# New planned times for every step of a two-layer graph kernel (graph attention, then graph convolution)

## The chip, the core and the metric

The kernel runs on one core of a Trainium2 chip. The metric is device time in microseconds (us), the median of the runs; smaller is better. TensorE is called PE, VectorE DVE, ScalarE ACT, GpSimd POOL, and SyncE, which here only issues DMAs, SP.

## What is computed

`x` is 32 batches of 512 rows (C) by 1024 columns (N), all float32; `adj` is a 512 x 512 matrix.

```python
h = maximum(layernorm(x), 0)                 # over the 1024 columns
q, k = wq . h, wk . h                        # one number per column
scores[m, n] = leaky(q[n] + k[m], 0.01)
att = softmax(scores, over n)
agg[c, m] = sum_n h[c, n] att[m, n]
x = x + relu(adj @ agg + bm)                 # layer 0
h = maximum(layernorm(x), 0)
x = x + (adj * adj).T @ h + bias             # layer 1
```

## The kernel before, in words

Attention is not done as a 1024 x 1024 product. The score of a pair is the sum of two numbers bent at zero, so for a given m every n whose q lies above a threshold gets one exponential factor, and every n below it another. The kernel ranks the 1024 columns by q, writes the rows of V = (adj @ h).T to DRAM in the order of rank, forms running sums over the sorted rows from both ends, and then each column m looks up where it stands in the order and picks three rows with one gather.

The work of one batch is cut into about 180 **steps**, each a small function that issues a few instructions:

- `load`, `stats0`, `norm0`, `slopes0`, `relu0`: x in four tiles of 128 x 1024; bn_stats on DVE, square root and relu on ACT.
- `scores` (PE, L349, 32-column products), ACT copies the result and DMAs it to DRAM; `row` (L360) reads it back broadcast to all partitions; `columns` (L365, L370) transposes it.
- `value` (L454): eight steps of four 128 x 512 float32 products each (two PE instructions per product); `spread` copies V to SBUF.
- `rank` (DVE, L391, L396, L400), `to_rows`: ranks and row numbers; `scatter` (POOL, L467) writes V's rows to DRAM in order of rank; `fetch` (SP, L484) reads them back sorted.
- `lower` (ACT, L407), `from_rows` (DVE, L437 to L447): where each column m stands.
- `weights` (ACT, L493, L496), `later` (DVE, L504, L508), `totals` (PE, L516, L517, then the copy of the denominators, L521), `stationary` (POOL, L527): weights of the sorted rows and the triangular matrices of the running sums.
- `scan` and `sums`, nine each: one step of the running sums. The two directions run in the two column halves of the array as 128 x 64 products (L543); in the fifth step (i = 4) both directions read the same block of rows, and one 128 x 128 product does it (L540). `sums` (ACT) copies two carry rows into the next blocks (L552, L553), which the next `scan` needs, then the sum itself (L555, L556), and SP stores it (L558, L559).
- `gather` (POOL, L564), `excess`, `divide`, `weigh` (ACT, L589), `combine` (DVE, 16 steps, L593): the three picked rows become one. `turn0`, `turn1` (L600): PE transposes back, four steps each, and DVE adds to x (L602).
- `stats1`, `norm1`, `slopes1`, `relu1`, `lift`: layer norm of layer 1. `propagate` (L607): eight steps of four products; `finish` (L615) adds on DVE, and SP stores the output.

What sets the order is a table. `PLAN` gives each step of a batch a time; batch b's are shifted by b * T. `FIRST` and `LAST` give the first five and last five batches a shift and a stretch for each kind of step. All steps of all batches are sorted by these times and issued in that order, so each engine has one fixed list that it runs from the front; what an engine waits for, everything behind it on that engine waits for too. The times are used for nothing else.

```python
times = PLAN[name]
mean = sum(times) / len(times)
...
t = s.b * T + t + shift + stretch * (t - mean)
steps.append((t, len(steps), f, (s, *lead, *(args[n] if args else (n,)))))
...
steps.sort(key=lambda e: e[:2])
with tc.manual_schedule():
    for _, _, f, args in steps:
        f(*args)
```

Buffers that bind neighbouring batches: 8 PSUM banks for all products, one buffer for the gathered rows (of 788 KB a gather step), five for the sorted rows (three a batch), two for sums on their way to DRAM, seven each for x and y tiles, eight for V.

Of the kernel before, what the change touches and what calls it, by code (L numbers as in the profile page):

```python
# [27 lines left out]
    "adjacency": (-107.86,),  # L28
    "biases": (73.25,),
    "columns": (2.54,),  # L30
    "combine": (
        293.1, 294, 295.37, 296.17, 294.24, 294.54, 295.16, 296.42, 294.48,
        294.66, 293.61, 295.28, 294.87, 296.68, 296.01, 296.52,
    ),
    "compare_mask": (-77.25,),
    "divide": (278.91,),
    "excess": (272.83,),
    "factors": (28.83,),
    "fetch": (74.87,),
    "finish": (357.8, 362.86, 376.29, 376.42, 388.63, 415.81, 401.13, 417.85),  # L40
    "from_rows": (89.36,),
    "gather": (250.12, 258.6, 255.35, 261.49, 268.91, 253.59, 258.29, 256.1),
    "later": (82.34,),
    "lift": (341.79, 343.89, 354.9, 347.45),
    "load": (-125.04, -82.54, -104.22, -58.22),
    "lower": (26.37, 18.82, 14.83, 28.33, 13.66, 12.67, 46.5, 36.18),
    "masks": (-12.78,),
    "norm0": (-27.69,),
    "norm1": (323.91,),
    "pads": (1.15,),  # L50
    "propagate": (347.57, 348.71, 350.13, 365.41, 372.81, 382.23, 382.61, 392.3),
    "rank": (16.85, 14.2, 18.53, 15.82, 17.42, 21.57, 23.3, 23.64),
    "reload": (275.48, 285.03, 274.13, 289.84),
    "relu0": (-17.18, -15.69, -15.67, -14.84),
    "relu1": (334.79, 335.4, 335.54, 338.3),
    "row": (1.98,),
    "scan": (89.28, 94.78, 102.87, 122.08, 139.17, 152.12, 172.91, 183.19, 200.42),
    "scatter": (39.55, 42.53, 43.86, 40.7, 49.58, 45.37, 44.59, 45.6),
    "scores": (-1.83,),
    "slopes0": (-22.22,),  # L60
    "slopes1": (324.32,),
    "spread": (10.78, 16.46, 5.24, 10.37, 28.25, 25.74, 19.08, 20.35),
    "square": (53.38,),
    "stationary": (83.36, 116.24, 162.19),
    "stats0": (-63.29, -60.88, -63.05, -41.14),
    "stats1": (318.79, 319.93, 319.41, 319.38),
    "sums": (89.92, 97.06, 115.14, 127.32, 141.99, 156.22, 174.86, 189.46, 207.26),
    "to_rows": (23, 29.08),
    "totals": (88.21,),
    "turn0": (303.69, 304.68, 304.05, 304.98),  # L70
    "turn1": (312.19, 312.02, 311.8, 312.15),
    "turn_adjacency": (-39.9,),
    "value": (3.89, 14.52, -1.07, 4.1, 20.69, 18.74, 15.77, 15.86),
    "weigh": (286.66, 289.32, 286.94, 289.3, 287.24, 286.87, 287.56, 291.05),
    "weights": (79,),
}
FIRST = {
    "columns": ((-37.98, 0), (-10.89, 0), (-8.73, 0), (-1.59, 0), (-5.53, 0)),
    "combine": ((-1.47, -0.283), (2.11, 0.074), (6.02, -0.446), (-3.46, 1.643), (-3.02, -0.662)),
    "divide": ((0.43, 0), (-4.84, 0), (5.31, 0), (-0.36, 0), (-5, 0)),  # L80
    "excess": ((6.36, 0), (0.71, 0), (9.39, 0), (2.63, 0), (1.02, 0)),
    "factors": ((14.45, 0), (42.49, 0), (37.13, 0), (-13.47, 0), (3.3, 0)),
    "fetch": ((-0.33, 0), (-9.12, 0), (-3.14, 0), (-6.37, 0), (-4.73, 0)),
    "finish": ((0.35, -0.506), (-4.34, -0.255), (-1.3, 0.166), (-13.48, -0.751), (-1, -0.145)),
    "from_rows": ((-17.73, 0), (122.52, 0), (-12.48, 0), (-3.68, 0), (39.28, 0)),
    "gather": ((-3.91, 0.337), (8.03, -0.392), (-0.23, 0.924), (1.48, -0.818), (-10.72, 0.312)),
    "later": ((-6.32, 0), (-2.49, 0), (-5.11, 0), (-3.44, 0), (5.07, 0)),
    "lift": ((5.78, 0.249), (-7.64, -0.77), (14.78, 1.406), (9.87, -0.096), (12.09, 1.113)),
    "load": ((-114.53, -0.719), (-41.9, -0.581), (-61.5, -0.134), (-67.36, 0.974), (-10.03, 0.381)),
    "lower": ((-4.18, -0.847), (-10.86, -0.761), (3.36, -0.598), (31.38, 0.125), (27.64, -0.444)),  # L90
    "norm0": ((-48.85, 0), (-42.24, 0), (-15.97, 0), (-23.37, 0), (-5.52, 0)),
    "norm1": ((-4.55, 0), (0.86, 0), (5.16, 0), (-3.3, 0), (2.66, 0)),
    "propagate": ((3.18, -0.698), (0.66, -0.203), (-2.02, -0.096), (-5.59, -0.325), (1.62, -0.11)),
    "rank": ((-4.4, 0.497), (1.55, -0.098), (-9.21, 1.126), (4.42, 0.365), (7.2, -0.023)),
    "reload": ((2.37, 0.404), (2.84, 0.512), (6.15, -0.047), (4.83, 0.053), (5.08, 0.729)),
    "relu0": ((-52.67, -0.811), (-32.9, 0.887), (-5.05, 1.412), (-5.92, -0.277), (0.27, -0.952)),
    "relu1": ((4.34, 0.844), (-4.2, 0.375), (9.88, -0.496), (1.58, 0.346), (-1.74, -0.782)),
    "row": ((-2.93, 0), (-19.24, 0), (-8.82, 0), (3.92, 0), (-1.39, 0)),
    "scan": ((-8.07, -0.009), (-4.12, 0.027), (-4.42, -0.075), (-2.52, 0.062), (-0.12, -0.002)),
    "scatter": ((19.59, 0.356), (0.39, -0.164), (-11.93, -0.276), (15.6, -0.115), (8.6, 0.613)),  # L100
    "scores": ((-48.13, 0), (-16.76, 0), (-5.07, 0), (-5.89, 0), (-6.97, 0)),
    "slopes0": ((-51.56, 0), (-32.21, 0), (-9.48, 0), (-3.65, 0), (3.28, 0)),
    "slopes1": ((3.12, 0), (1.34, 0), (13.39, 0), (3.58, 0), (5.29, 0)),
    "spread": ((3.65, -0.128), (-4.12, 0.811), (6.73, -0.135), (3.45, 0.185), (7.08, 1.002)),
    "stationary": ((-16.55, -0.278), (-1, 0.017), (-1.03, 0.007), (-4.23, -0.058), (4.88, -0.025)),
    "stats0": ((-86.5, 0.491), (-55.52, 0.533), (-26.5, 0.735), (-39.6, 0.274), (-0.81, 0.405)),
    "stats1": ((-2.32, 0.867), (-1.78, -0.548), (-2.88, 0.916), (-1.4, -0.748), (0.94, 0.179)),
    "sums": ((-4.03, -0.009), (-3.78, 0.04), (-3.01, -0.086), (-3.05, 0.043), (0.68, 0.024)),
    "to_rows": ((-6.46, 0.165), (-1.64, -0.568), (-5.7, -0.361), (5.62, -0.493), (8.82, -0.906)),
    "totals": ((-7.21, 0), (-4.95, 0), (-6.35, 0), (-3.7, 0), (-0, 0)),  # L110
    "turn0": ((1.54, 1.026), (5.01, 1.316), (7.07, -0.842), (11.23, 1.597), (7.25, 0.74)),
    "turn1": ((-5.63, 2.282), (4.23, 0.277), (-3.42, -0.878), (-9.56, -0.462), (0.94, 1.931)),
    "value": ((-14.35, 0.282), (-16.49, 0.638), (-1.63, 0.411), (-4.93, 0.45), (-4.23, 0.018)),
    "weigh": ((-1.72, 0.361), (-2.31, -0.775), (10.15, 0.018), (-5.33, 0.803), (-1.65, 0.186)),
    "weights": ((-3.94, 0), (-0.72, 0), (-2.63, 0), (-0.65, 0), (3.83, 0)),
}
LAST = {
    "columns": ((4.26, 0), (-3.03, 0), (2.37, 0), (-0.77, 0), (3.86, 0)),
    "combine": ((164.15, 0.268), (7.89, -0.595), (-1.54, 0.851), (5.2, 1.047), (1.56, -0.96)),
    "divide": ((162.11, 0), (3.32, 0), (-8.28, 0), (1.71, 0), (-3.58, 0)),  # L120
    "excess": ((127.64, 0), (-3.09, 0), (-3.12, 0), (2.67, 0), (0.92, 0)),
    "factors": ((-11.15, 0), (-18.33, 0), (1.07, 0), (-11.1, 0), (-11.56, 0)),
    "fetch": ((-1.81, 0), (-1.04, 0), (-0.37, 0), (-0.32, 0), (-3.1, 0)),
    "finish": ((699.4, -0.546), (150.27, -0.075), (20.88, 0.53), (4.22, 0.22), (6.11, 0.071)),
    "from_rows": ((13.84, 0), (-28.23, 0), (48.43, 0), (-17.87, 0), (17.41, 0)),
    "gather": ((88.35, 0.017), (-13.92, -0.31), (-9.45, 0.61), (-5.67, 0.718), (-2.02, 0.573)),
    "later": ((7.83, 0), (2.55, 0), (2.21, 0), (-1.95, 0), (-0.28, 0)),
    "lift": ((585.22, -0.837), (120.6, 0.105), (1.56, -0.183), (-6.91, -0.419), (9.05, -0.044)),
    "load": ((1.51, 0.156), (-2.49, 0.009), (4.84, -0.047), (9.16, -0.437), (7.85, -0.154)),
    "lower": ((9.16, 0.14), (-5.44, 0.016), (-5.91, -0.205), (-2.69, 0.118), (-12.14, -0.652)),  # L130
    "norm0": ((-2.04, 0), (-6.51, 0), (-2.65, 0), (-11.04, 0), (5.36, 0)),
    "norm1": ((418.29, 0), (27.36, 0), (-0.04, 0), (-2.45, 0), (1.02, 0)),
    "propagate": ((526.78, -0.74), (151.44, 0.764), (12.38, 0.445), (9.65, 0.206), (11.26, 0.117)),
    "rank": ((4.79, 0.609), (3.43, 0.076), (-8.9, -0.909), (-5.02, -0.932), (1.67, 0.09)),
    "reload": ((184.29, -0.585), (23.97, -0.873), (-3.56, 0.841), (1.54, 0.226), (-3.06, -0.231)),
# [27 lines left out]
def kernel(  # L163
# [457 lines left out]
    T = 80.4  # L621
# [77 lines left out]
```

## Time and profile before

| what | number |
|---|---|
| median of 3 runs (lowest to highest) | 2385.05 us (2382.75 to 2387.69) |
| the profiled execution | 2390.79 us |
| its span, first to last instruction | 2389.1 us |
| mean granted clock of PE | 0.985 |
| DMA traffic | 643.45 MB, 269 GB/s |
| start of `scores` of batches 0, 1, 2, 3, 4, 5, 6, 7 | 14.3, 53.1, 105.9, 158.9, 219.0, 293.2, 370.6, 441.3 us |
| start of `scores` of batches 28, 29, 30, 31 | 1929.5, 2004.8, 2076.9, 2140.5 us |
| from one start to the next, batches 10 to 26 | 70.5 to 71.1 us |

How to read the views: the page gives each engine's busy time and its share of the span, and rows of 40 digits, the busy tenths in 40 equal slices. The waits list who waited for whom: total, number, longest. The timeline lists instructions in order of time: start, duration, engine, line, operation, written and read tiles, and in brackets the engine's idle time before it and what ended it. A 128 x 512 product of PE is two instructions that start 0.43 us apart.

### The profile page before, as it was taken

What the parts mean: (1) busy time and instruction counts of PE and PEld (TensorE: products, weight loads), DVE (VectorE), ACT (ScalarE), POOL (GpSimd) and SP (SyncE); (2) the same over time, 40 slices, a digit from 0 to 9 for tenths busy, and PEclk for the clock granted to TensorE, in tenths of its full rate; (3) what the DMA queues carried; (4) which work ended last, traced back from release to release, by engine and by line L of the source; (5) the groups of instructions that cost most, each with busy time, mean ns of one, the idle gap of its engine ahead of it and who ended that gap; (6) DMA issues with size and microseconds to landing.
All of it is one profiled execution on the core that took longest, in us unless ns stands there. A gap on an engine that the chain in (4) does not pass through costs nothing.

```text
span 2389.1 us, 28172 instructions
## 1 busy us (share of the span) xinstructions
PE 2298.7 (96%) x7568; PEld 1016.2 (43%) x7568; DVE 1957.4 (82%) x5008; ACT 1589.4 (67%) x2878; POOL 719.5 (30%) x973
## 2 busy tenths in 40 slices
PE   7787999999999999999999999999999999999897
PEld 3233434444444444444444444444444444444343
DVE  6457978788988888988888898888898878889675
ACT  4576666766776766776676677676676856676450
POOL 2233323232332233233223233223323233223310
PEclk9898999999999999999999999999999999999898
DMA  7679887988988998988998888899998888988872
GB/s 231 154 188 279 275 286 256 302 256 269 300 284 284 289 293 258 290 294 268 293 305 261 272 291 285 285 289 282 273 281 277 281 279 250 290 267 282 290 294 87
DMA packets 206895, 643.45 MB, mean 269 GB/s; under 512 B 29120, under 2 KB 29248, under 8 KB 206736
## 3 DMA queue, kind: packets, MB, share of 16 engines
q1 hardware_dynamic: 142944, 355.74, 52.3%
q0 software_dynamic: 57344, 268.99, 30.9%
q10 hardware_dynamic: 6448, 16.92, 2.2%
q8 instruction: 61, 1.00, 0.2%
q14 instruction: 98, 0.80, 0.1%
HBM read 429.94 MB, written 211.60 MB: 269 GB/s over the span
## 4 chain that ended last, share of the span: by engine, by line
PE 84%; DMA 7%; DVE 4%; ACT 3%; issue 1%; SPq 1%; POOL 0%; ACTq 0%; DVEq 0%; POOLq 0%
PE pg L607 35%; PE pv L454 31%; PE sc L543 10%; PE tr L600 4%; DMA vs<-td 3%; PE pq L349 2%; DMA td<-t 2%; PE sc L540 1%; DVE g L593 1%; DVE st L319 1%; DMA qd<-qr 1%; DVE junk L396 1%; DMA wqk<-in_L_gnn_wk_dram 1%; DMA g<-td,idg 1%; SPq L484 0%
## 5 line engine op out<-in xcount | busy, mean ns | idle before, releaser
L607 PE MATMUL pg<-h,wsq 128*128 128x512 f32 x2048 | 908.4, 597 | 12.1 <-ACT h L337 11.9
L454 PE MATMUL pv<-wmT,x 128*128 128x512 f32 x2048 | 906.5, 597 | 1.1 <-ACT x L337 1.0
L607 PEld LDWEIGHTS pg<-h,wsq 128*128 128x128 f32 x2048 | 382.6, 190 | 513.3 <-issue 475.9
L454 PEld LDWEIGHTS pv<-wmT,x 128*128 128x128 f32 x2048 | 381.8, 191 | 495.8 <-issue 457.6
L527 POOL TENSOR_TENSOR sm<-mask_a,wc 128x192 f32<-128x192 f32 x96 | 57.3, 596 | 1128.5 <-DVE wc L504 718.8
L593 DVE SCALAR_TENSOR_TENSOR g<-g,cf 128x512 f32<-128x512 f32 x512 | 363.2, 777 | 6.4 <-ACT g L589 3.6
L467 POOL DMA_INDIRECT td<-v,idx x256 | 285.1, 1114 | 251.7 <-POOL v L466 41.4
L564 POOL DMA_INDIRECT g<-td,idg x256 | 244.0, 953 | 193.9 <-issue 67.9
L543 PE MATMUL sc<-vs,sm 128*64 128x512 f32 x1024 | 287.5, 629 | 12.5 <-ACT vs L552 4.9
L407 ACT ACTIVATE junk<-qrow,qk 128x1024 bf16<-128x1024 f32 x256 | 294.7, 1151 | 6.3 <-DVE qk L370 2.9
L552 ACT COPY vs<-sc 1x512 f32<-1x512 f32 x256 | 145.1, 567 | 214.4 <-PE sc L543 150.3
L602 DVE SCALAR_TENSOR_TENSOR y<-tr,nbm,y 128x512 f32<-128x512 f32 x256 | 176.0, 743 | 56.7 <-PE tr L600 52.0
L615 DVE SCALAR_TENSOR_TENSOR y<-pg,bm_sb,y 128x512 f32<-128x512 f32 x256 | 186.2, 734 | 34.4 <-PE pg L607 34.4
L555 ACT COPY t<-sc 128x512 f32<-128x512 f32 x288 | 168.3, 585 | 66.4 <-DMA td<-t 49.7
L396 DVE TENSOR_SCALAR_CACHE_REDUCE junk<-qrow,qk,cnt 128x896 bf16<-128x896 f32 (+6 forms) x224 | 180.4, 805 | 8.2
L337 ACT ACTIVATE x<-x,nmr,rstd 128x1024 f32<-128x1024 f32 x128 | 148.8, 1231 | 38.4 <-DVE nmr L330 38.4
L391 DVE TENSOR_SCALAR_CACHE_REDUCE junk<-qrow,qk 128x128 bf16<-128x128 f32 (+6 forms) x224 | 164.9, 736 | 8.2 <-issue 2.4
L461 ACT COPY v<-pv 128x512 f32<-128x512 f32 x256 | 140.6, 583 | 44.8 <-issue 28.3
L319 DVE BATCH_NORM_STATS2 st<-x 128x6 f32<-128x512 f32 x256 | 162.1, 675 | 7.1 <-DMA x<-in_x_dram 7.1
L589 ACT ACTIVATE g<-g,cf 128x512 f32<-128x512 f32 x256 | 163.4, 712 | 1.9 <-DVE cf L583 1.9
L343 DVE TENSOR_TENSOR y<-y,bias_sb 128x1024 f32<-128x1024 f32 x128 | 156.6, 1230 | 7.9 <-ACT h L337 7.9
L319 DVE BATCH_NORM_STATS2 st<-y 128x6 f32<-128x512 f32 x256 | 159.1, 663 | 0.0
(111 smaller groups left out, 1913.3 us busy)
## 6 DMA issues: line engine op xcount, KB each, us to landing
vs<-td SPq DMA_DIRECT2D x192, 384.8 KB
td<-t SPq DMA_DIRECT2D x576, 128.2 KB
x<-in_x_dram SPq DMA_DIRECT2D x128, 512.0 KB
y<-in_x_dram SPq DMA_DIRECT2D x128, 512.0 KB
out_dram<-y SPq DMA_DIRECT2D x128, 512.0 KB
qrow<-qd ACTq DMA_DIRECT2D x32, 512.0 KB
td<-v,idx POOLq DMA_INDIRECT x256, 8.3
g<-td,idg POOLq DMA_INDIRECT x256, 13.4
```

The source lines that it names most:

```text
L319: nc.vector.bn_stats(st[:, i, :], s.x[c][:, ts(i, HALF)])
L396: nc.vector.tensor_scalar(junk[:, j * P :], s.qrow[:, j * P :], qc, first, ALU.is_lt, ALU.add, accum_out=s.cnt[:, 1, j : j + 1],)
L407: nc.scalar.activation(junk, s.qrow, AF.Sign, bias=s.qk[:, 1, j : j + 1], accum_out=s.sgn[:, j : j + 1])
L454: nc.tensor.matmul(pv, s.h[c][:, ts(j, P)], wmT[:, c, :], start=(c == 0), stop=(c == NC - 1))
L467: i = nc.gpsimd.indirect_dma_start(tds[s.b % TABLES][:, :], bass.IndirectOffsetOnAxis(ap=s.idx[j // 4][:, j % 4 : j % 4 + 1], axis=0), v[: ...
L543: nc.tensor.matmul(p[ts(k, HP), :], m[:, k, :], s.vs[h][:, 0:C], start=True, stop=True)
L555: nc.scalar.copy(t[:, 0:C], p)
L564: nc.gpsimd.indirect_dma_start(s.g[:, j, :], None, tds[s.b % TABLES][0 : 3 * NB * HP, :].rearrange("(s k) w -> s (k w)", k=3), bass.Indire ...
L593: nc.vector.scalar_tensor_tensor(r, s.g[:, j, k * W : k * W + C], s.cf[:, k, j : j + 1], r, ALU.mult, ALU.add)
L602: nc.vector.scalar_tensor_tensor(xh, pt, nbm[:, o : o + 1], xh, ALU.max, ALU.add)
L607: nc.tensor.matmul(pg, wsq[:, r, ts(c, P)], s.h[r][:, ts(i, HALF)], start=(r == 0), stop=(r == NC - 1),)
L615: nc.vector.scalar_tensor_tensor(xh, s.pg.pop((c, i)), bm_sb[:, c : c + 1], xh, ALU.add, ALU.add)
```

## The change

Only numbers change: all times in `PLAN`, all shifts and stretches in `FIRST` and `LAST`, and T. No step is added, removed or altered; the instructions are the same, and so is the fifth sum as one product, which both kernels have. What differs is the order in which each engine finds its work.

```diff
 PLAN = {
...
     "combine": (
-        293.1, 294, 295.37, 296.17, 294.24, 294.54, 295.16, 296.42, 294.48,
-        294.66, 293.61, 295.28, 294.87, 296.68, 296.01, 296.52,
+        295.023, 296.8619, 296.7183, 298.4701, 293.1697, 294.7416, 294.2429, 299.1951, 298.6716,
+        299.3937, 297.2442, 298.3468, 299.3257, 299.415, 296.3588, 297.6774,
     ),
...
-    "from_rows": (89.36,),
+    "from_rows": (87.779,),
...
-    "later": (82.34,),
+    "later": (82.6454,),
...
-    "propagate": (347.57, 348.71, 350.13, 365.41, 372.81, 382.23, 382.61, 392.3),
+    "propagate": (345.5459, 348.74, 351.3718, 365.8954, 370.5235, 381.8844, 381.5713, 389.3079),
...
-    "scan": (89.28, 94.78, 102.87, 122.08, 139.17, 152.12, 172.91, 183.19, 200.42),
+    "scan": (
+        88.7256, 94.0816, 102.8865, 119.4156, 135.2128, 151.5405, 171.0515, 183.5338, 198.3883,
+    ),
...
 FIRST = {
...
-    "propagate": ((3.18, -0.698), (0.66, -0.203), (-2.02, -0.096), (-5.59, -0.325), (1.62, -0.11)),
+    "propagate": (
+        (3.9127, -0.68976), (4.3839, -0.23748), (-0.2269, -0.34495), (-0.0128, -0.28129), (3.8198, -0.06573),
+    ),
...
 LAST = {
...
-    "weights": ((1.5, 0), (-0.48, 0), (3.89, 0), (-1.19, 0), (0.73, 0)),
+    "weights": ((5.3666, 0), (-4.6466, 0), (0.3996, 0), (-6.5338, 0), (2.7794, 0)),
 }
...
-    T = 80.4
+    T = 80.6473
```

The resulting order of PE in the middle of the run, from one batch's scores to the next (batch b; the numbers are the steps' indices):

```
before                                after
scores b                              scores b
value b: 2                            value b: 2
columns b                             columns b
value b: 0 3                          value b: 3 0
totals b-1                            totals b-1
scan b-1: 0, b-2: 6, b-1: 1           scan b-1: 0, b-2: 6, b-1: 1
value b: 1 6 7 5 4                    value b: 1 6 7 5 4
scan b-2: 7, b-1: 2                   scan b-2: 7, b-1: 2
propagate b-4: 00 01 10               propagate b-4: 00 01 10
scan b-2: 8, b-1: 3                   scan b-2: 8, b-1: 3
propagate b-4: 11 20                  propagate b-4: 11 20
scan b-1: 4 (one product)             scan b-1: 4 (one product)
propagate b-4: 21 30                  propagate b-4: 30 21
turn0 b-3: 0 2 1 3, turn1: 2          turn0 b-3: 0 2 1 3
propagate b-4: 31                     propagate b-4: 31
turn1 b-3: 1 3 0                      turn1 b-3: 3 2 1 0
scan b-1: 5                           scan b-1: 5
```

## The prediction

> **What bounds the kernel now.** I read the page first, then TensorE's waits in the ramp and at the end, then stretches of the span, then the timeline around the waits.
>
> The page says that TensorE (PE) is the bound, and that what it lacks lies in the first and last slices:
>
> ```profile
> span 2389.1 us, 28172 instructions
> PE 2298.7 (96%) x7568; PEld 1016.2 (43%) x7568; DVE 1957.4 (82%) x5008; ACT 1589.4 (67%) x2878; POOL 719.5 (30%) x973
> PE   7787999999999999999999999999999999999897
> ```
>
> The stretches (columns: length, busy time of PE, PEld, DVE, ACT, POOL with counts, granted clock, DMA share, GB/s) put numbers to it. Between 700 and 1850 us PE is idle 0.2 us in 1150, at full clock. In the first 239 us it is idle 50 us and runs at 0.89 to 0.94 in three of four stretches; in the last 309 us it is idle 27 us.
>
> ```profile
> 59.70:119.50 59.80, 46.41 (x137) 17.72 (x135) 26.05 (x90) 35.05 (x71) 12.31 (x22) 0.89 0.68 155
> 179.20:238.90 59.70, 44.93 (x169) 19.69 (x169) 46.55 (x139) 41.01 (x80) 19.75 (x28) 0.89 0.91 279
> 700.00:1850.00 1150.00, 1149.77 (x3840) 511.70 (x3838) 1001.07 (x2537) 810.87 (x1470) 364.15 (x489) 1.00 0.90 282
> 2080.00:2240.00 160.00, 150.03 (x472) 65.76 (x472) 128.91 (x340) 108.21 (x206) 53.96 (x71) 0.96 0.89 282
> ```
>
> PE's waits to 530 us, then from 1850 us (total, times, longest), name the ends of its idle time: `totals` waiting for the weights (L493, which wait for the sorted rows, `fetch`), and `scan` waiting for the carries (L552, L553) that ACT copies.
>
> ```profile
> PE pd L516 <- ACT w L493: 14.0, 5, 4.8
> PE sc L540 <- ACT vs L553: 11.7, 3, 7.7
> PE tr L600 <- DVE g L593: 4.4, 1, 4.4
> ...
> PE pg L607 <- ACT h L337: 11.9, 2, 10.7
> PE pd L516 <- ACT w L493: 9.6, 2, 7.5
> PE sc L543 <- ACT vs L552: 3.1, 2, 2.3
> ```
>
> **The change, part by part.** No instruction is added or removed; only the order on the five engines changes. I count steps from the sorted plans of both kernels and price them by the trace.
>
> *The loop (batches 5 to 26, 22 of 32).* PE's list of a loop holds the same steps in both: scores, 8 values, totals, 9 scans, 8 propagates, 8 turns. Half-column groups per loop stay 4 (scores adjoin a scan). A batch's scores start 70.5 us after the last one's (1221.3, 1291.8), with no wait, so the loop can only get worse, by a new wait. The tightest cover is the first turn: DVE runs without idle from the copy of the denominators at 1234.36 to the 14th `combine`, near 1283.2, and the turn starts at 1283.8: 0.6 us. In the new order the 12 small `from_rows` instructions (1234.44 to 1236.95, 2.5 us) go ahead of that copy, into the 3.0 us in which DVE waits for PE anyway, and the turn needs 13 combines, not 14 (0.66). Everything else between is the same set. Slack becomes 0.6 + 2.5 + 0.7 = 3.8 us. `later` now stands behind `columns`, whose transpose ends at 1227.1, before the weights (1229.1): no cost, and `totals` at 1233.9 keeps some 4 us. Loop: 0.
>
> *Batch 4's totals.* Here the trace has
>
> ```profile
> 284.18 1.02 PE L540 MATMUL sc<-vs,sm 128*128 128x512 f32 x2
> 285.04 3.59 PE L607 MATMUL pg<-h,wsq 128*128 128x512 f32 x8
> ...
> 308.63 0.38 PE L516 MATMUL pd<-w,mask_a 128*64 128x9 f32 x2 [2.77 <-ACT w L493]
> 311.21 0.28 PE L517 MATMUL pd<-e,ones 128*64 128x9 f32 x1 [2.20 <-DVE e L508]
> ```
>
> SP issues `fetch` 4 behind the stores of the fifth sum (the L540 product). From that product to the release are 311.2 - 284.2 = 27.0 us; PE had work for 22. The new order moves two propagates (3.44 each, 8 instructions at 0.43) and one scan (0.94) behind the product: 22 + 7.8 = 29.8, above 27.0. The 5.0 us go. Ends: -5 and 0 (if `fetch` 4 waits for its scatters instead; those come earlier, since `to_rows` 4 moves ahead of `excess` and `divide` 1).
>
> *Batches 0 to 2 (to 180 us).* Waits of totals and scans sum to 19 us (4.8, 4.1, 4.1, 4.0, 2.2). Earlier now: `stats0` of batch 2's last tile leaves the middle of batch 1's ranks (2 x 0.66 + 0.2 = 1.5); `to_rows` 1 starts after four ranks, not six; the square-root step of batch 2 (1.28 table load + 0.30) no longer precedes a carry copy. Later: the `relu` of batch 1 stand behind all eight `spread` of batch 0 (about +1.2). The first 14.3 us are untouched. I take -3; ends -7 and +3.
>
> *The knot at 198 to 213 us (7.75 + 4.38).* The carry of batch 2's fourth sum stood on ACT behind five `weigh`, three `lower` and another sum; now behind three `weigh` (0.64 each): the product starts some 5 us earlier. But the sixth scan now stands ahead of the turns, and its carry is behind five more `weigh`, the root, a sum and a `lower`: about 3.1 + 1.6 + 0.8 + 1.3 + 1.2 = 8 us. By then the turns wait no more (`combine` 0 also loses the 2.5 us of `from_rows` 1 in its middle). So 7.75 - 5 + 8 = 10.8 in place of 12.1: -1.3; ends -6 and +4. Batch 3's totals (2.64, the wait for `sm`) get one more scan ahead of them and earlier weights: -1.5; ends -2.6 and 0. Batch 8's (1.8): -0.5; ends -1.8 and +3.
>
> *Clock.* After the knot 31 turns take 5.25 us; 32 take 3.66 where the clock is full. Section "Part 1: The HAM clock gate" of "TensorE: Matmul & The Clock Gate" in the Trainium skill says that an idle window of about 3.4 us halves the clock until a busy one has passed. By the bare waits the ramp gains 5 + 3 + 1.3 + 1.5 + 0.5 = 11.3; by that rule each long wait that goes brings up to 1.7 us more. Only the 5 us one goes whole, and the others shrink, so +2; ends 0 and 4. Ramp: -13.3.
>
> *Last batches.* Three waits near 1893, 1944 and 2018 to 2022 (5.7 in all): -1; ends -5.7 and +5. Batch 31's totals wait 7.5. Its chain gets shorter (the row of scores no longer waits on ACT behind batch 30's weights, issued at 2155.7 where the scores were ready at 2142.8), but PE has a propagate and eight turns less ahead of it (3.4 + 3.8), and `fetch` 31 again meets the gathers (its last part came 20 us after the issue): -1; ends -7.5 and +6. The 2.25 us between batch 31's first scans: propagates of 3.44 now stand between them and cover copies of 1.2: -2; ends -2.25 and 0. The last 10.7 us (turns, DVE, relu of batch 31 ahead of the last propagates) keep their order: 0. End: -4.
>
> *Half columns.* "TensorEngine Tiling (Array Packing)", section "Key Properties", says that changing the tiling mode drains TensorE. The trace shows what that is worth: a product before a half-column group takes 522 ns start to start, not 429, and one after it 533: 0.2 us a visit. The change speaks of fewer visits, but I count 133 groups of half-column products in the old order and 134 in the new: +0.2 by the row; by the change's own words it would be a gain.
>
> *New waits.* A new order makes waits that this trace can't show: 0 to 12 us. I take 4, somewhat less than the 5.7 that three late batches, whose order is the loop's with shifts, show here.
>
> Sum: -13.3 - 4 + 0.2 + 4 = -13.1. The profiled execution took 2390.8 us (its span and 1.7 around it), 0.24% above the median of the runs, 2385.05. 2390.8 - 13.1 = 2377.7, and on the median's scale (0.9976 of it) 2372.0.
>
> **Rivals.** *Larger gain (0.20):* the waits go as the far ends say: ramp -5 - 7 - 6 - 2.6 - 1.8 - 4, end -15.5: -42 with no new waits, of which some 30 may be had together: 2355. For it: most waits are order, not work. Against: the chain scores, rank, scatter, fetch is as long as before.
> *Moved, not removed (0.10):* the knot keeps its 12 us under another name (the sixth scan behind `weigh`: +1.3), batches 0 to 2 keep theirs (+3), and new waits are 10, not 4 (+6): 2382. For it: the eight us worked out above.
> *Slower (0.08):* the loop gets a wait. Place: SP's queue. The load of batch b+3's first tile now stands right behind that of batch b+2's last, ahead of the stores of batch b-1's eighth sum, not after them. A load stands until a tile of x is free: SP waits there for values (L306 <- PE pv L454) 54 us in 25 times. Behind it are the stores, and ACT has only two tiles for sums, so a late store stops ACT (it waits 2.4 us a loop for one now), then carries and scans. In the trace the four tiles of a batch come free with its last value, the first at 1252.4, when SP issues the earlier load, the last at 1254.9; the stores are due at 1258.5. So it decides once the tile comes over 3.6 us later than the last value. Each us beyond costs 22 us: one gives 2372 + 22 = 2394. Against: nothing after the last value reads x.
>
> **How the numbers follow.** Forecast 0.62, the rivals 0.20, 0.10 and 0.08. Range 2352 to 2382.5: it reaches through the larger gain and most of the moved case. The measurement can tell about 0.2% (4.8 us) from no change; forecast and larger gain are faster than that: 0.82; moved is within: 0.10; slower 0.08.
>
> **What would show it.** Right: PE idle 0 between 700 and 1850 and starts of batches 70.5 us apart; no wait of totals near 300; PE idle before 330 us down from 55 to about 44; the wait before batch 31's scans gone, that before its totals still 5 us or more; the last wait 10.7. Wrong: a PE wait repeated in each loop, or a ramp with as much idle as before.

## The result and the profile after

| | before | after |
|---|---|---|
| median of 13 runs each (lowest to highest) | 2389.28 us (2382.75 to 2397.0) | 2376.68 us (2372.45 to 2381.76) |
| the profiled execution, its span | 2390.79, 2389.1 us | 2375.1, 2373.4 us |

The ratio is 0.9953, with a 95% interval of 0.9939 to 0.9967: 11.2 us less by the ratio (the two medians lie 12.6 us apart). I had forecast 13.1 us, a ratio of 0.9945, inside this interval. In the new kernel all line numbers are 94 higher (L516 is L610, L540 is L634, L543 is L637). First the page of after, then two of its stretches (length, busy time of PE, PEld, DVE, ACT and POOL with counts, granted clock, DMA share, GB/s):

```profile
span 2373.4 us, 28107 instructions
PE 2292.0 (97%) x7568; PEld 1011.3 (43%) x7568; DVE 1956.9 (82%) x5008; ACT 1603.1 (68%) x2882; POOL 725.4 (31%) x973
```
```profile
179.20:238.90 59.70, 43.17 (x158) 19.70 (x157) 42.91 (x124) 40.28 (x79) 19.18 (x26) 0.84 0.92 273
700.00:1850.00 1150.00, 1149.88 (x3880) 511.38 (x3879) 994.08 (x2529) 815.68 (x1462) 358.73 (x480) 1.00 0.90 283
```

The middle is as full as it was. In the first 239 us PE is idle as long as before (50 us before, 53 now), which I had not expected. To 330 us I had expected a fall from 55 to about 44 us; here it is 53. A ramp with as much idle as before was one of my two signs of being wrong; more executions follow below. The waits of PE to 530 us, then from 1850 us:

```profile
PE pd L610 <- ACT w L587: 14.4, 3, 8.0
PE sc L637 <- ACT vs L646: 7.7, 3, 5.5
PE sc L634 <- ACT vs L647: 7.2, 3, 4.5
```
```profile
PE pd L610 <- ACT w L587: 6.2, 1, 6.2
PE sc L637 <- ACT vs L646: 3.0, 1, 3.0
```

Fewer waits, but longer ones: totals waited 14.0 us in five pieces, now 14.4 in three. To see where the 15.7 us between the two spans went, I cut both executions at the scores of batches 9, 26 and 30. Before:

```profile
0.00:585.70 585.70, 528.79 (x1734) 229.12 (x1734) 437.61 (x1215) 386.71 (x707) 176.58 (x253) 0.97 0.82 250
...
1785.90:2076.90 291.00, 285.00 (x946) 126.27 (x947) 241.42 (x624) 199.49 (x360) 92.09 (x120) 0.99 0.90 276
2076.90:2389.10 312.20, 284.90 (x883) 127.24 (x882) 235.57 (x519) 157.26 (x281) 71.03 (x90) 0.95 0.73 244
```

After:

```profile
0.00:577.70 577.70, 524.25 (x1738) 227.82 (x1739) 440.54 (x1214) 390.18 (x709) 176.46 (x253) 0.97 0.84 255
...
1777.00:2058.80 281.80, 281.80 (x947) 124.80 (x945) 243.53 (x625) 201.68 (x361) 95.93 (x120) 1.00 0.90 279
2058.80:2373.40 314.60, 286.75 (x880) 127.13 (x878) 236.79 (x518) 158.51 (x282) 70.75 (x90) 0.96 0.74 246
```

Read by length: -8.0 in the ramp, -0.9 in 17 loops, -9.2 in the late batches, +2.4 in the tail. Both loops take 1200 us (1200.2 and 1199.3, left out here). From this pair I took as my **theory** that the gain is made at both ends, half each. **Rivals**: that it lies in the loop, by fewer visits to column halves, as the change says of itself; and that waits are only moved, because the chain of each batch (scores, ranks, scatter, fetch) sets them.

### The profile page after: what moved, and what is told of

It is laid out like the page before. It is cut to its first block, busy times and chain, and to the rows that moved or that the text cites. A ratio compares the mean times of both kernels' runs of the same rounds, so it can differ in the third digit from the quotient of the medians.

```text
span 2373.4 us, 28107 instructions
## 1 busy us (share of the span) xinstructions
PE 2292.0 (97%) x7568; PEld 1011.3 (43%) x7568; DVE 1956.9 (82%) x5008; ACT 1603.1 (68%) x2882; POOL 725.4 (31%) x973
## 4 chain that ended last, share of the span: by engine, by line
PE 89%; DMA 5%; DVE 2%; ACT 1%; POOL 1%; issue 1%; SPq 0%; ACTq 0%; POOLq 0%; DVEq 0%
PE pg L701 37%; PE pv L548 34%; PE sc L637 10%; PE tr L694 4%; PE pq L443 2%; DMA vs<-td 2%; PE sc L634 1%; DMA td<-v,idx 1%; DMA g<-td,idg 1%; DVE st L413 1%; DMA qrow<-qd 1%; DMA qd<-qr 1%; POOL td L561 0%; DMA x<-in_x_dram 0%; ACT x L431 0%
## 5 line engine op out<-in xcount | busy, mean ns | idle before, releaser
L687 DVE SCALAR_TENSOR_TENSOR g<-g,cf 128x512 f32<-128x512 f32 x512 | 358.1, 764 | 38.8 <-ACT g L683 35.3
L561 POOL DMA_INDIRECT td<-v,idx x256 | 292.7, 1144 | 136.6 <-POOL v L560 38.1
L637 PE MATMUL sc<-vs,sm 128*64 128x512 f32 x1024 | 284.4, 624 | 14.8 <-ACT vs L646 10.7
L490 DVE TENSOR_SCALAR_CACHE_REDUCE junk<-qrow,qk,cnt 128x640 bf16<-128x640 f32 (+6 forms) x224 | 180.4, 806 | 8.2
L485 DVE TENSOR_SCALAR_CACHE_REDUCE junk<-qrow,qk 128x384 bf16<-128x384 f32 (+6 forms) x224 | 165.6, 739 | 5.6
L555 ACT COPY v<-pv 128x512 f32<-128x512 f32 x256 | 145.4, 583 | 31.6 <-PE pv L548 12.3
```

Source lines behind the costliest of these rows:

```text
L490: nc.vector.tensor_scalar(junk[:, j * P :], s.qrow[:, j * P :], qc, first, ALU.is_lt, ALU.add, accum_out=s.cnt[:, 1, j : j + 1],)
L561: i = nc.gpsimd.indirect_dma_start(tds[s.b % TABLES][:, :], bass.IndirectOffsetOnAxis(ap=s.idx[j // 4][:, j % 4 : j % 4 + 1], axis=0), v[: ...
L637: nc.tensor.matmul(p[ts(k, HP), :], m[:, k, :], s.vs[h][:, 0:C], start=True, stop=True)
L687: nc.vector.scalar_tensor_tensor(r, s.g[:, j, k * W : k * W + C], s.cf[:, k, j : j + 1], r, ALU.mult, ALU.add)
```

## The experiments

All times are against the kernel before, run on the same chip; 0.9953 is the new kernel. A difference in us is worked out from the ratio; the plain medians lie up to some 2 us from it. In the edits `ahead(a, b)` takes step a out of the sorted list and puts it right in front of b, `behind(a, b)` right after it; nothing else changes.

**p_ramp, p_loop, p_late: the new times for some batches only.** The old tables stand beside the new ones, and a batch in NEW takes its times from the new ones; the shifts by T or by the old T (T_0) are added up to match.

```diff
+NEW = range(0, 9)            # p_loop: range(9, 24); p_late: range(24, 32)
...
-        times = PLAN[name]
+        new = s.b in NEW
+        PLAN_, FIRST_, LAST_ = (PLAN, FIRST, LAST) if new else (PLAN_0, FIRST_0, LAST_0)
+        times = PLAN_[name]
```

> Batches 0 to 8 are issued by the new times, batches 9 to 31 by the old ones. Theory (the gain is made at the two ends of the run, and the loop has no part in it): the scores of batch 9 start 8 us earlier in the new kernel's trace, and this kernel keeps that gain to its end: 8 us less than before, ratio 0.9965. Rival (the gain comes from the order in the loop, by fewer visits to column halves): at most a third of it, 0 to -3 us, ratio 0.999 to 1.0.

> Batches 9 to 23 are issued by the new times, all others by the old ones. Theory (ends of the run): within 1 us of before, ratio 1.000; starts of batches stay 70.5 us apart. Rival (the loop gains by fewer visits): 15 of 22 loops are new, so at least half of the 11 us, -5 us or more, ratio 0.998 or less. A third way, that the two joints between the orders cost waits: +1 to +4 us, and then the trace shows them near the scores of batches 9 and 24 only.

> Batches 24 to 31 are issued by the new times, batches 0 to 23 by the old ones. Theory (ends of the run): the stretch from the scores of batch 26 to those of batch 30 is 9 us shorter in the new kernel's trace and the tail 2 us longer: -7 us, ratio 0.997, and the three waits between 1890 and 2025 us are gone. My prediction gave the late batches only -1 and the tail -3. Rival (loop): 0 to -3 us.

Measured: p_ramp 2380.74 us, ratio 0.9976 (0.9964 to 0.9988), -5.7; p_loop 2397.57, 1.0036 (1.0021 to 1.0052), +8.6; p_late 2401.09, 1.0057 (1.0037 to 1.0077), +13.6. Away from the joints the starts of batches stay 70.5 us apart in all three, under either order. The joints cost more than the parts are worth: p_late takes 1212.4 us from the scores of batch 9 to those of 26 where before takes 1200.1, p_loop 1208.0, p_ramp 1201.5. Where batches 23 and 24 meet in p_late:

```profile
1643.81 6.44 PE L834 MATMUL pg<-h,wsq 128*128 128x512 f32 x8 [4.78 <-ACT t L782]
```

A propagate waits for ACT, where neither order alone has a wait, and runs at half clock after it (6.44 us for 8 instructions, not 3.60). So p_ramp shows that the order of the ramp alone is worth about half of the gain (its trace reaches the scores of batch 9 at 578.9 us, and loses 1.4 us of that at its joint). p_loop shows that the loop's period is not the gain. p_late decides nothing: its own late batches are faster, but less than its joint is slower. What the end is worth is shown by no run of its own.

**product: the step for batch 4's totals, alone.**

```diff
+    ahead(("scan", 3, 4), ("propagate", 0, 2, 1))
+    ahead(("sums", 3, 4), ("lower", 4, 3))
```

> The kernel before, with one product moved: the fifth sum of batch 3 goes two propagates earlier on TensorE, and its copies ahead of one lower on ScalarE, as my step for batch 4's totals had it. By that step (fetch 4 waits for the stores of this sum): the wait of 5.0 us before batch 4's totals goes, -5 us, and up to -1.7 more by the clock: ratio 0.997 to 0.998. Rival (fetch 4 waits for its scatters, the last of which is issued until 281.4 us, and in the new kernel fetch 4 comes 8.0 us after its last scatter): fetch 4 stays at 289 us, the wait stays at 4 to 5 us: 0 to -1 us, ratio 1.000.

Measured: 2383.02 us, ratio 0.9982 (0.9966 to 0.9997), -4.3. Its SP queue and PE (start, duration):

```profile
282.98 0.46 SPq L558 DMA_DIRECT2D td<-t  x1
286.51 8.12 SPq L484 DMA_DIRECT2D vs<-td  x6
```
```profile
309.72 0.22 PE L517 MATMUL pd<-e,ones 128*64 128x9 f32 x1 [1.68 <-DVE e L508]
```

The sum is stored at 283.0 (287.1 before), fetch 4 follows at 286.5 (289.2), and the wait of 5.0 us is down to 1.7. The last scatter was issued until 282.4, so 4 us after it are enough: the scatters did not hold the fetch. My step for this wait stands. But the same trace waits 2.7 us before the totals of batch 7, with 6.8 us at half clock, and so reaches the scores of batch 9 no earlier than before (587.5 us). The time's interval excludes no change only just; see three_moves.

**late_moves, late_rows, late_rows_2, three_moves: the late batches, step by step.** All are the kernel before with moves:

```diff
# late_moves
+    ahead(("weights", 27), ("row", 28))
+    behind(("to_rows", 28, 1), ("rank", 28, 7))
+    behind(("to_rows", 28, 0), ("rank", 28, 7))
# late_rows (three_moves: with product's two lines)
+    for b in (27, 28):
+        behind(("to_rows", b, 1), ("rank", b, 7))
+        behind(("to_rows", b, 0), ("rank", b, 7))
# late_rows_2: late_rows and
+    for j in (3, 1, 7):
+        ahead(("weigh", 25, j), ("sums", 26, 8))
```

> The kernel before, with three steps moved: batch 27's weights go ahead of batch 28's row on ScalarE (the row's transfer waits there for the scores in DRAM, and the weights behind it), and both to_rows of batch 28 go right behind its last rank on VectorE, 13.6 us earlier (fetch 28 waited 9.3 us for the scatters). Theory (these two places are the late batches' loss): the waits of 2.08 + 0.29 and of 0.85 + 1.64 go, and one half-clock window of 3.4 us with them (1.7): -5 to -6.5 us, ratio 0.9975, and batches 26 to 30 start 70.5 to 71.5 us apart. Rival (the late transfers are slow by themselves): the waits stay under other names, 0 to -1.5 us, ratio 1.000.

Measured: 2400.23 us, ratio 1.0054 (1.0037 to 1.007), +12.9. I had misread which wait came last: the fetch had not landed. The weights now waited for it on ACT until 1944.7, the row's transfer and a sum behind them, that sum's store and an x tile's load behind those on SP, a stats0 on DVE for this tile until 1955.9, and the copy of the denominators behind the stats0. ACT then shows

```profile
1957.45 0.19 ACT L556 COPY t<-den 128x1 f32<-128x1 f32 x1 [4.26 <-DVE den L521]
```

and PE waited 6.3 us in four places between 1949 and 1966. The batch took 83.9 us. (Its tail was some 10 us longer too, which I did not follow.)

> The kernel before, with the two to_rows of batches 27 and 28 right behind the last rank on VectorE, and nothing else. In the trace of before, the first scatter comes 37.6 us after a batch's scores in the loop, but 49.5 and 51.6 us after them in batches 27 and 28, and their fetch 4 to 10 us later than in the loop; in the new kernel 42.7 and 38.9. Theory (this sets the late waits): both fetches come 61 to 65 us after the scores, batches 27 to 29 start 70.5 to 71 us apart instead of 73.1 and 75.2, and the waits near 1944 and 2018 are gone: -5 to -7 us, ratio 0.9975. Rival (what late_moves showed, that a later x tile or row stands in the way as well): the start of batches stays 73 us or more apart, 0 to -2 us, ratio 1.000.

Measured: 2388.29 us, ratio 0.9999 (0.9985 to 1.0012). The cause is right in part. Fetches 27 and 28 are issued 65.4 and 68.6 us after the scores (70.4 and 73.3 in the trace of before), later than I wrote, and batch 27's totals wait 1.0 us, not 2.4. But the 70.9 us from the scores of batch 27 to those of 28, in place of 73.1, are not the move's: product and p_ramp, which have the old order there, take 70.9 without it. From 28 to 29 it takes 77.3 us, where the old order has 73.7 to 75.2 (before, product, p_ramp), and from 29 to 30 it takes 69.3, where the old order has 72.1 to 74.2. In the slower interval:

```profile
1989.45 0.58 ACT L555 COPY t<-sc 128x512 f32<-128x512 f32 x1 [5.77 <-DMA td<-t]
```

ACT has two tiles for sums, and waits for an earlier one to reach DRAM; three weigh, the combine steps and the first turn stand behind.

> late_rows, with three weigh of batch 25 ahead of two sums on ScalarE. In late_rows batch 27's interval fell from 73.1 to 70.9 us, but the next one rose to 77.3: ScalarE waited 5.8 us for the store of an earlier sum (its waits for such stores rose from 6.1 to 14.4 us, since the earlier scatters now meet the stores), the three weigh stood behind it, and combine and the first turn behind them (2.4 us, and a half-clock window). Theory (that wait is the whole loss, and it matters only for what stands behind it): with the weigh ahead, the interval is 72 to 73.5, and the time 3 to 5 us below before, ratio 0.998 to 0.9987. Rival (the stores are late for the carries as well, since ScalarE now reaches them later): the fifth sum's product or the scans wait instead, the interval stays at 76 us or more, ratio 1.000.

Measured: 2385.43 us, ratio 0.9995 (0.9981 to 1.0009). The turn's wait is gone, but the interval is 74.8, between the two theories: with the same to_rows moves the totals of batch 27 wait 2.2 us here, nearly as long as in before, and 3.4 us at half clock follow. The next interval has a wait of 1.6 us (den, behind stats0). The time is that of before.

> The kernel before, with the moves of product and of late_rows together: the fifth sum of batch 3 two propagates earlier, and the to_rows of batches 27 and 28 behind their ranks. If the gain of the new times lies in these places, the two add up: -4 from product and -5 from late_rows, -9 us, ratio 0.996, against 0.9953 for all new times. If the new times gain in many small places, or in the loop, this stays at -4, ratio 0.998.

Measured: 2386.94 us, ratio 0.9991 (0.9972 to 1.0011). It does not reach -9. That fits the rival, "many small places" (-4), better, though not to show it; and it leaves product's -4.3 in doubt: with the same move this one is 2.1 us below before, and its ramp is no shorter (588.2 us to the scores of batch 9, 585.7 in before). A single stall can be taken out of this order with three lines; the time cannot.

**values_first: is the ramp bound by order or by the chain?**

```diff
+    for j in (1, 6):
+        ahead(("value", 2, j), ("totals", 1))
```

> The new kernel, with two values of batch 2 (3.56 us each) ahead of batch 1's totals on TensorE, which waits there 8.0 us for the sorted rows. If that wait is only a matter of TensorE's order: -7 us against the new kernel, ratio to before 0.9925. If the ramp is bound by the chain of each batch (scores, ranks, scatter, fetch) and TensorE has too little other work: the 7 us return before the totals of batches 2 and 3 or at the knot near 200 us, 0 to -2 us, ratio 0.9945 to 0.9953, with TensorE's idle time before 240 us unchanged at 53 us.

Measured: 2377.86 us, ratio 0.9965 (0.9953 to 0.9977): not better than the new kernel. Its waits of PE to 240 us (totals had 14.4, scans 7.7 and 7.2):

```profile
PE sc L637 <- ACT vs L646: 13.1, 5, 5.5
PE sc L634 <- ACT vs L647: 8.0, 3, 4.4
PE pd L610 <- ACT w L587: 6.7, 2, 6.2
```

The 8.0 us wait is 0.5, and a carry of 3.8 us appears right behind. (The 13.1 us hold another 1.65 that the new kernel has too, put down there to ACT's square root, L418.) PE's idle time to 239 us is 49.3 us, not 53 as I wrote; but late_fix and late_fix_2 below, with the new kernel's order there, have 48.1 and 50.2, so this fall is not shown to be the move's. The scores of batch 3 start at 158.7 us (158.1 in the new kernel), those of batch 4 at 214.4 (213.2 to 215.6 in the new order). The second theory holds: the filled wait is not won.

**two_visits: the price of a visit to column halves.**

```diff
+    for b in range(5, 27):
+        ahead(("scan", b - 2, 7), ("value", b, 4))
+        ahead(("scan", b - 2, 8), ("propagate", b - 4, 1, 0))
```

> The new kernel, with two more visits to column halves in each of 22 loops: the eighth and the ninth sum of the older batch go one value and one propagate earlier on TensorE, so that groups of four half-column products become two groups of two. By the price that I took from the trace (0.2 us a visit): 70.5 becomes 70.9 us a loop, +9 us against the new kernel, ratio to before 0.999. Rival (the price is hidden, or is one of the group and not of the change): 0 to +2 us, ratio 0.995 to 0.996. A new wait of TensorE in the loop would spoil it; the carries have 3.4 us less cover out of 17.

Measured: 2392.99 us, ratio 1.0029 (1.0018 to 1.0041): 0.0076 above the new kernel's, 18 us for 44 visits, about twice my price. The loop takes 71.2 us in place of 70.5 with PE never idle (22 loops make 15 of the 18 us). A whole group in the new kernel, then one of its halves here:

```profile
1245.98 1.94 PE L637 MATMUL sc<-vs,sm 128*64 128x512 f32 x8
1247.85 10.57 PE L701 MATMUL pg<-h,wsq 128*128 128x512 f32 x24
```
```profile
1250.80 1.08 PE L637 MATMUL sc<-vs,sm 128*64 128x512 f32 x4
1251.81 3.70 PE L548 MATMUL pv<-wmT,x 128*128 128x512 f32 x8
```

From the start of the group to the next product it is 1.87 us for eight instructions, and 1.01 for four: 0.15 more for two groups. That is the part I had missed; with 0.09 and 0.10 on the products before and after it makes the 0.35 us a visit that the loop shows (0.7 for two). The new order has one visit more than the old, so this is not where it gains.

**late_fix, late_fix_2: batch 31's totals.**

```diff
+    for j in (5, 4, 2):
+        behind(("lower", 31, j), ("sums", 29, 6))
+    ahead(("scan", 30, 5), ("turn", 28, 0, 0))
+    ahead(("fetch", 31), ("sums", 30, 4))        # late_fix only
+    behind(("factors", 31), ("to_rows", 31, 1))
```

> The new kernel, with six steps of the last batches moved: three lower of batch 31 go behind the seventh sum of batch 29 on ScalarE (its carry stood behind a lower that waits 4.8 us for the row); batch 30's sixth sum goes ahead of eight turns on TensorE (the third part of fetch 31 waits for its tile); fetch 31 goes ahead of the fifth sum's stores, and factors 31 behind both to_rows. Theory (the chain of batch 31 sets its totals, and the buffer of the third part ends it): the wait of 3.0 us at 2159 goes, and batch 31's totals are released 3 to 4 us earlier, so that their wait stays near 6: -3 to -5 us against the new kernel, ratio to before 0.9935. Rival (the fetch is slow by the gathers beside it, whenever it is issued): the 3.0 us are added to the wait before the totals, 0 to -1 us, ratio 0.995.

Measured: 2378.89 us, ratio 0.9969 (0.9956 to 0.9983), 0.0016 above the new kernel's, with intervals that overlap. The line of the fetch made it overtake a scatter: 128 rows of batch 31 are read before they are written, so this kernel leaves out an order that the result needs. The scatter waits:

```profile
2205.24 0.98 POOL L561 DMA_INDIRECT td<-v,idx  x1 [25.52 <-DMA td<-t]
```

> The new kernel, with the moves of late_fix but for the one of the fetch: there it went ahead of the last scatter in the program, so it read rows that were not yet written, the scatter waited for it (25 us on GpSimd), and two scans waited 2.5 and 6.5 us for what stands behind it. Now it stays behind all scatters. Theory (the third part of fetch 31 waits for the tile that batch 30's sixth sum reads): the 3.0 us wait at 2159 is down to 1.2 as in late_fix, the third part is issued at 62 to 63 us after the scores and not 65.2, and batch 31's totals 80 us after them and not 82.9: -2 to -4 us against the new kernel, ratio to before 0.994. Rival (the totals wait for the fetch's rows beside the gathers, whenever they are asked for): totals stay at 82 to 83 us, 0 to -1 us, ratio 0.995.

Measured: 2374.41 us, ratio 0.9934 (0.9911 to 0.9957), against the new kernel's 0.9953 (0.9939 to 0.9967): the best median of all, but the intervals overlap, and it is not shown to be faster. Its trace does what the theory said and more: no wait near 2157 us, the third part of the fetch 61.0 us after the scores (65.2), the totals 78.5 us after them (82.9).

```profile
2209.19 0.38 PE L610 MATMUL pd<-w,mask_a 128*64 128x9 f32 x2 [5.38 <-ACT w L587]
```

The last product ends at 2366.8 us (2368.6): of the 3.6 us won at the totals, 1.8 are left.

## Why the prediction was right, point by point

The first theory fell in part. Executions of one order differ by 6 us and more in a stretch, and the pair of profiles was an uneven one. The runs above give more executions; I took for each stretch all those whose order in it is that of before or of after. Starts of scores, means (lowest to highest, number):

| from scores of batch | old order | new order | difference |
|---|---|---|---|
| start to 4 | 218.0 (215.2 to 221.7, 8) | 213.8 (212.2 to 215.6, 5) | -4.2 |
| 4 to 9 | 368.9 (366.8 to 370.6, 5) | 362.5 (362.1 to 363.3, 4) | -6.4 |
| 9 to 26 | 1199.9 (1199.4 to 1200.5, 6) | 1199.1 (1198.9 to 1199.3, 4) | -0.8 |
| 26 to 30 | 290.0 (288.7 to 291.0, 3) | 282.8 (281.8 to 284.1, 4) | -7.2 |
| 30 to the last product | 306.7 (301.4 to 316.7, 8) | 310.8 (309.8 to 312.1, 4) | +4.1 |

They sum to -14.5, beside the -11.2 of the runs; so few executions give no better. (The 221.7 and the 316.7 are late_moves; without it the tail is +5.5 and the sum about -13.) The ramp is worth about 10 us. Of the 7 us that the late batches gain, the tail gives most back: in the executions that keep one order from batch 26 to the end, the whole end takes 594.5 us (591.8 to 598.5, 3) and 591.9 (591.6 and 592.1), some 3 us less and hardly outside the spread. p_ramp puts the ramp at 5.7 us (2.9 to 8.6 by its interval), rather less than the table.

- **The loop (0).** Right: no wait, 70.5 us. The slower rival (a late x tile) did not appear.
- **Batch 4's totals (-5).** The wait is gone in every execution of the new order, and product shows its cause: the sum's stores, not the scatters. What it is worth in the end is not shown, since in product the time was lost again at batch 7's totals.
- **The knot (10.8 in place of 12.1).** Right to the tenth, but by luck. The new trace has the two waits that I had worked out, and 0.8 us ahead of them:

```profile
200.50 2.07 PE L634 MATMUL sc<-vs,sm 128*128 128x512 f32 x2 [4.51 <-ACT vs L647]
208.05 2.57 PE L637 MATMUL sc<-vs,sm 128*64 128x512 f32 x4 [5.47 <-ACT vs L646]
```

  I had put the first at 7.75 - 5 = 2.75 us and the second at 8; with the 0.8 counted to the first, two errors of 2.5 us cancelled. The three sum to 10.6 to 12.2 us in five executions of the new order, and to 12.0 to 12.9 in eight of the old: most of the knot stayed.
- **Batches 0 to 2 (-3), batch 3's totals (-1.5).** The first is about right, the second is wrong. In the profile of after, batch 1's totals wait 8.0 us where before had 3.8, but other executions of the new order have 2.4 to 5.5. In the mean of the executions in the table's first row, the totals of batches 0 to 2 wait 9.6 us in the old order and 6.4 in the new, and the scores of batch 3 start at 158.6 and 156.2 us. Batch 3's totals, or the scan beside them, waited 1.9 to 3.9 us in the old order; in the new one they wait 5.8 to 7.9, in each execution. In after:

```profile
234.95 0.39 PE L610 MATMUL pd<-w,mask_a 128*64 128x9 f32 x2 [5.58 <-ACT w L587]
```

  Its weights waited on ACT until 234.6 us for the third part of a fetch that was issued by 221.8. I had counted what PE reaches sooner and not what releases it. This wait, 3.7 us longer in the mean, is most of the "new waits" that I put at +4 without a place.
- **Batch 8's (-0.5).** This wait, before batch 7's totals near 525 us, was worth more: 0.5 to 3.6 us in seven executions of the old order, none in after, late_fix, late_fix_2 and values_first.
- **The ramp in all (-13.3).** PE's idle time to the scores of batch 9 is 56.4 us before and 50.6 after (means of the five and three executions with one order all the way there): -5.8, where the terms said -11.3 and new waits of 4. To 330 us it falls from 54.0 to 50.6, by 3 us and not by 11; this is nearer to my sign of being wrong than to the forecast. Time at half clock is 43.7 and 37.6 us, which is worth 3.1, a little more than my 2. The two make 9 of the ramp's 10 us.
- **Late batches (-1) and tail (-3).** The mis-sized terms: -7.2 and +4.1 (the new order has one scan, 0.9 us, more in the fourth stretch and one less in the fifth; else each stretch holds the same products). The three waits all went in the new trace (PE is idle 0.0 us from 1777 to 2059). In the tail the wait before batch 31's scans went, as forecast (2.25 us), and its totals wait 6.2; but a new wait of 3.0 came at 2159, a carry behind a lower that waited for the row. That does not account for the tail, whose other waits shrank or grew with the execution; what makes it longer is open.
- **Half columns (+0.2).** The trace of after has the one group more that I had counted; the price is 0.35 us and not 0.2.

No rival came as a whole: no kernel of the new order is near 2355 us, and the loop got no wait. "Moved, not removed" is true of most of the knot, but its 2382 us, a ratio of 0.9987, lies outside the interval. In sum: terms of -17.3, +0.2 and +4 had errors that cancelled, late batches against tail and ramp waits against new ones. The total was right in part by luck.

## What to carry to other kernels

A wait in a ramp belongs to what releases it: before counting a filled wait as gained, ask whether the release moves too (values_first: 7.5 us filled, nothing won). When an order is found as a whole, its parts are not worth what they seem alone: moves that cure one stall wake the next one behind it, and a joint of two good orders can cost 12 us. And for effects below 1%, compare stretches over several executions of the same order before naming a place; one pair of profiles put 7 us at the end of the run, where the means put 3.

## What the hardware showed that I had not expected

A short wait can cost more than itself by the clock. The old order waits for batch 7's totals near 527 us; in two executions with that same order there, the wait differs by 0.3 us (the seventh number is the granted clock). First three_moves, with a wait of 2.56 us, then late_rows_2, with 2.26:

```profile
520.00:535.00 15.00, 12.21 (x34) 5.40 (x33) 9.73 (x37) 8.87 (x18) 5.85 (x8) 0.77 0.96 268
```
```profile
520.00:535.00 15.00, 12.44 (x40) 4.87 (x39) 9.34 (x38) 9.92 (x19) 6.34 (x8) 1.00 0.91 264
```

The first then ran 6.8 us at half clock, and that batch took 76.9 us, not 74.7. Waits of 2.67 and 3.37 us there did the same; 0.2 to 1.1 us brought no window at half clock. But the length alone does not decide: before batch 27's totals, waits of 1.9 to 2.1 us brought 3.4 us at half clock in four executions (before, p_ramp, late_rows_2, three_moves), and waits of 2.0 and 2.2 us brought none in p_loop and product. The Trainium skill's "TensorE: Matmul & The Clock Gate", section "Part 1: The HAM clock gate", speaks of an idle window of about 3.4 us; here 1.9 us could be enough, and 2.26 us were not always. What else decides is not shown here.
